# Softmax denominators in a fused attention and state-space kernel: halves of the weight sums added across partitions before the products

## The chip, the cores and the metric

The kernel runs on one core of a Trainium2 chip. The metric is device time in microseconds (us) from launch to end, as the median of a few executions on the chip. A core has five engines with queues of their own: TensorE (PE) for matrix products, VectorE (DVE), ScalarE (ACT), GpSimd (POOL), and SyncE (SP), which here only issues DMAs. Each engine takes its instructions strictly in the order written; between engines, semaphores make an instruction wait for what it needs. PSUM is the memory that TensorE writes to, in eight banks of 128 partitions by 512 fp32 numbers; SBUF is the working memory of 128 partitions.

## What is computed

Cross attention of 4096 queries over 3202 keys with 8 heads of 64, a residual, a layer norm, a linear recurrence with SiLU of 64 states over the 4096 rows, and a second residual with a constant row. All in fp32. Cut to what matters:

```
x      = layernorm(builder_state, g1, beta1)
base_n = layernorm(base_state, g1, beta1)
q, k, v = heads of x, base_n, base_n              # 8 heads of 64
scores = einsum('bhqd,bhkd->bhqk', q, k) / sqrt(64)
attn   = softmax(scores, axis=-1)
out    = einsum('bhqk,bhkd->bhqd', attn, v)
x      = builder_state + out @ W_o.T + b_o
u      = (layernorm(x, g2, beta2) @ W_in.T + b_in) @ Bmat
s      = silu(s @ A.T) + u_t                      # for each row t
return x + states @ Cmat + mod
```

The change concerns the denominator of the softmax alone: the sum over all keys of exp(score), for each query and head.

## The kernel before

**Units and steps.** After a first stage that makes keys and values (up to about 230 us), the work is cut into 64 *units*. A unit is (Q, hp, half): a block Q of 512 queries (eight of them), a pair hp of heads (four), and a half of the block, that is 256 queries (QU). A tile's name carries these three numbers, as acc_2_0_1. The last block takes all pairs of half 0 first and then those of half 1, so the last unit is (7, 3, 1). A unit has 13 *steps* (NDC), one for two chunks of 128 keys (the last one has one chunk).

**A step.** `scores` (L643) makes for both heads (index a) and both chunks (index b) the scores of 128 keys (partitions) by 256 queries, in eight products of 64 by 64 by 256. The array is used as four quarters of 64 rows by 64 columns, so four such products run side by side. The result lies in a PSUM tile `s` of two banks, of which there are two. `weights` (L713) is ScalarE's exp from there into an SBUF tile `p` of 128 x 1024 (18 buffers, the planner's ring "p"). `add` (L721) is VectorE's running sum of the `p` tiles into `acc` (128 keys x 2 heads x 2 chunks x 256 queries, three buffers). `product` (L753) multiplies the weights by the values some four steps later; the halves of its contraction (keys 0 to 63 and 64 to 127 of each chunk) go to two PSUM banks of `po`. 64 keys that do not fill a chunk are handled apart: `sample`, `maximum`, `spread`, `base` (which also find the shift of the exponentials), `extra`, `rest` (L707) and the first products of L741, which have 128 columns.

**The end of a unit** is in `finish`. `output` (L788, ScalarE) copies one bank of `po` to SBUF and `join` (L792, VectorE) adds the other. `fold` (L728, VectorE) adds the two chunks of `acc`. `sums` (L771, TensorE) multiplies by ones: for each head and each half of the partitions one product of 64 by 64 by 256, the two halves to two banks `pd`. `denominators` (L805, ScalarE) reads both banks, copies the first into the SBUF tile `rd`, and sums each over the queries for a check (`rises`). `whole` (L809, VectorE) adds the second bank into `rd`. `inverse` (L812), `scale` (L819) and `fall` (L815), all on VectorE, take the reciprocal, scale the output and sum up for the check. For the last unit `sums` writes to a tile of the `s` ring (pd_last) instead of to two "m" banks.

**What sets the order.** All of this is written as pieces with an engine, a cost, pieces that have to come before, a due time, and the rings (buffers) that a piece takes and gives back. `Plan.order` runs through modelled time and takes on each free engine the ready piece with the earliest due time. `LATE` is how long after its end another engine sees a piece's result; `PORT` lists VectorE's pieces that may not run beside GpSimd's. The order that comes out is the order in every engine's queue. On the chip nothing is reordered: a piece that isn't ready holds up what stands behind it.

**The rings.** "m": two PSUM banks, shared by pd, by the projections (`heads` L320, `outs` L997, `inputs` L1053) and transposes; near the end `first_scan` takes both for the first sweep of the recurrence (za). "s": the two score tiles. "acc": three buffers; a unit's goes back when its `sums` is done. "rd": two buffers.

**The end of the kernel.** Row products (yb, L1343) of the last 256 queries, then two recurrences at once: a sweep over 128 pieces of rows (L1187, L1215, L1222) with its output rows (L1261 to L1286), and one over the last rows (L1425, L1428).

The pieces around the change, before:

Of the kernel before, what the change touches and what calls it, by code (L numbers as in the profile page):

```python
# [10 lines left out]
F32 = mybir.dt.float32  # L11
# [9 lines left out]
P = 128  # L21
TB = 32
# [45 lines left out]
class Plan:  # L68
# [6 lines left out]

    LATE = {"PE": 110, "DVE": 500, "ACT": 110, "POOL": 100, "SP": 5000}
    ENTER, LEAVE = 110, 147
    KEEP, ALONE = 6000, 30000
    PORT = ("add", "rest", "fold", "scale")

# [98 lines left out]
def xattn_ssm_kernel(  # L179
# [545 lines left out]
    def fold(w):  # L725

        acc = w["acc"]
        nc.vector.tensor_tensor(acc[:, :, 0, :], acc[:, :, 0, :], acc[:, :, 1, :], ALU.add)  # L728

    def product(w, c):  # L730

# [30 lines left out]
    def sums(w):  # L762

        if w["last"]:
            both = ps_s.tile([P, 2, 512], F32, tag="s", name="pd_last")
            w["pd"] = [both[:, k] for k in range(2)]
        else:
            w["pd"] = [m_tile([P, 512], f"pd_{w['name']}_{k}") for k in range(2)]
        for a in range(2):
            for k, (k0, k1) in enumerate(((0, HD), (HD, P))):  # L770
                nc.tensor.matmul(  # L771
                    w["pd"][k][a * HD : (a + 1) * HD, :QU],
                    ones[k0:k1],
                    w["acc"][k0:k1, a, 0, :],
                    start=True,
                    stop=True,
                )
# [16 lines left out]
    def finish(w, i, d, plan):  # L794
# [5 lines left out]
        def denominators(k):  # L800
            if k == 0:
                w["rd"] = op.tile([P, QU], F32, tag="rd", name=f"rd_{name}", bufs=2)
            of = rows_of(w, w["pd"][k][:, :QU], True)
            to = of if k else rows_of(w, w["rd"])
            nc.scalar.activation(to, of, AF.Copy, accum_out=rises[:, 3 * i + k : 3 * i + k + 1])  # L805
# [11 lines left out]
        def scale(part):  # L817
# [6 lines left out]
        plan.add(("fold", i), "DVE", 680, partial(fold, w), [("add", i, NDC - 1)], d + 500)  # L824
        plan.add(("sums", i), "PE", 450, partial(sums, w),
                 [("fold", i)] + ([] if last else [from_(d + 2 * STEP)]), d + 1000,
                 ["s"] if last else ["m", "m"], [("acc", ("add", i, 1))], "quarters")
        for k in range(2):
            plan.add(("den", i, k), "ACT", 420, partial(denominators, k), [("den", i, 0) if k else ("sums", i)], d + 2500 + k,
                     [] if k else ["rd"], [(ring, ("sums", i))])  # L830
        plan.add(("whole", i), "DVE", 430, whole, [("den", i, 1)], d + 3000, [], [(ring, ("sums", i))])
        parts = [slice(t * P, (t + 1) * P) for t in range(2)] if last else [slice(0, QU)]
        for t, part in enumerate(parts):
            plan.add(("inverse", i, t), "DVE", 950 if last else 1750, partial(inverse, part),
                     [("whole", i)], d + 5000 + t)
            plan.add(("scale", i, t), "DVE", 400, partial(scale, part),
# [122 lines left out]
    def mixes(Q):  # L959
        return 0 < Q < NQB - 1  # L960
# [588 lines left out]
    def drain(plan):  # L1549
# [14 lines left out]
        plan.add("c2", "SP", 200, open_scan, [("heads", NQB - 1, NC - 1)], a0 - 6 * STEP, ["xn", "q"])  # L1564
        plan.add("open", "DVE", 600, first_scan, ["c2", ("whole", n - 4), *kept_], a0, ["m", "m"])
        for p in sweep("a", None, "end1", a0 + 1000, A_PACE, ["open"]):
            plan.add(*p)
        plan.add("start", "SP", 0, ready_scan, ["fetch", ("sums", n)], d - 2 * STEP, ["s"])
        plan.add("yb", "SP", 0, ready_rows, [("whole", n - 1)], a0, ["m", "m"])
        plan.add("py1", "SP", 0, ready_py, ["start", ("whole", n)], d, ["s"])  # L1570
# [324 lines left out]
```

## Time and profile before

| What | Value |
|---|---|
| Median of 3 runs | 2000.53 us (1997.67 to 2000.59) |
| Profiled execution | 2000.26 us, of which the span of its instructions is 1998.4 |
| Busy share of the span | PE 98%, DVE 72%, ACT 56%, POOL 12% |
| Keys and values, first queries (0 to 231 us) | PE busy 220.2, DVE 59.8, ACT 72.8 |
| Units up to the last block (231 to 1720 us) | PE busy 1483.6, DVE 1177.2, ACT 909.0 |
| Last block (1720 to 1936 us) | PE busy 212.7, DVE 169.4, ACT 128.0 |
| End (1936 to 1998.4 us) | PE busy 43.5, DVE 35.7, ACT 16.7, POOL 25.3 |

How to read the lines of the profile: `L771 PE MATMUL pd<-acc,ones 64*64 64x256 f32 x504 | 38.9, 376 | 0.0` is the group of instructions of line 771 on TensorE that write pd from acc and ones, in a 64 by 64 quarter with 256 columns, 504 of them; they were busy for 38.9 us together, one took 376 ns from its start to its modelled end, and the engine sat idle for 0.0 us before them. Four quarters overlap, and every fp32 product is recorded twice (two passes), so the pace is read from the chain in time, not from one instruction. PEld is the loading of weights into the array. In the chain, "issue" is time in which nothing that the profile shows was waited for.

### The profile page before, as it was taken

How to read it: one execution, taken by the hardware profiler on the slowest of the kernel's cores; microseconds unless marked ns; L12 is line 12 of the kernel's file. 1: busy time of each engine (PE TensorE's matmuls, PEld its weight loads, DVE VectorE, ACT ScalarE, POOL GpSimd, SP SyncE). 2: the span in 40 equal slices, each digit the busy share in tenths (PEclk: the TensorE clock that was granted, in tenths of full speed). 3: DMA queues.
4: the chain of work that ended last, by engine and by line, in shares of the span. 5: the costliest groups of instructions: out<-in, count | busy, mean ns of one | idle time of the engine just before them, and what ended most of it. 6: DMA issues, size and time to landing. Idle time of an engine off the chain costs nothing.

```text
span 1998.4 us, 66546 instructions
## 1 busy us (share of the span) xinstructions
PE 1959.9 (98%) x29070; PEld 1250.2 (63%) x29070; DVE 1442.1 (72%) x1786; ACT 1126.5 (56%) x1478; POOL 235.3 (12%) x378
## 2 busy tenths in 40 slices
PE   8999999999999999999999999999999999999996
PEld 4444566666666666666666666666666666666674
DVE  4311488687877788778868787779777886878675
ACT  2233467566656566556756565656655666655552
POOL 2111000002100120012100210012001100011014
PEclk9999999999999999999999999999999999999998
DMA  5632323223422243224412342234321331544475
GB/s 172 193 98 66 102 80 104 59 81 106 111 74 78 88 113 93 62 71 110 106 48 78 105 109 71 79 95 115 84 78 59 102 92 47 150 136 142 141 209 181
DMA packets 246935, 204.29 MB, mean 102 GB/s; under 512 B 80808, under 2 KB 220072, under 8 KB 246636
## 3 DMA queue, kind: packets, MB, share of 16 engines
q1 hardware_dynamic: 242088, 192.28, 33.3%
q10 hardware_dynamic: 4548, 7.67, 1.2%
q8 instruction: 231, 3.78, 0.8%
q14 instruction: 68, 0.56, 0.1%
HBM read 156.32 MB, written 29.88 MB: 93 GB/s over the span
## 4 chain that ended last, share of the span: by engine, by line
PE 95%; DVE 2%; ACT 1%; issue 1%; DMA 1%; SPq 0%; POOL 0%; ACTq 0%; DVEq 0%; POOLq 0%
PE s L643 35%; PE po L753 34%; PE pq L320 6%; PE pa L997 5%; PE pk L592 4%; PE pv L559 4%; PE pd L771 1%; ACT p L713 1%; PE pu L1053 1%; PE sm L661 1%; PE po L741 1%; PE tp_c L291 0%; PE za L1187 0%; DVE row L1281 0%; PE sm L680 0%
## 5 line engine op out<-in xcount | busy, mean ns | idle before, releaser
L713 ACT ACTIVATE p<-s,shifts 128x1024 f32<-128x1024 f32 (+1 forms) x832 | 885.4, 1080 | 552.2 <-PE s L643 543.4
L721 DVE TENSOR_TENSOR acc<-p,acc 128x1024 f32<-128x1024 f32 (+1 forms) x704 | 842.3, 1196 | 185.5 <-ACT p L713 146.0
L643 PE MATMUL s<-q,k 64*64 64x256 f32 x12800 | 831.4, 378 | 8.6 <-ACT p L713 7.5
L753 PE MATMUL po<-p,v 64*64 64x256 f32 x12800 | 813.3, 376 | 0.0
L643 PEld LDWEIGHTS s<-q,k 64*64 64x64 f32 x12800 | 477.8, 133 | 251.2 <-ACT p L713 54.8
L753 PEld LDWEIGHTS po<-p,v 64*64 64x64 f32 x12800 | 491.1, 133 | 187.8 <-issue 2.4
L991 POOL TENSOR_TENSOR xr<-xr,rowb 128x512 f32<-128x512 f32 x30 | 55.2, 1857 | 892.3 <-DMA xr<-in_x_dram 467.5
L721 DVE TENSOR_TENSOR acc<-p,p 128x1024 f32<-128x1024 f32 x64 | 82.5, 1288 | 69.6 <-ACT p L713 64.0
L320 PE MATMUL pq<-xn,wq 128*128 128x512 f32 x256 | 118.3, 605 | 0.0
L812 DVE RECIPROCAL rd<-rd 128x256 f32<-128x256 f32 (+1 forms) x65 | 112.4, 1729 | 2.2
L997 PE MATMUL pa<-wo,o 128*128 128x512 f32 x240 | 107.0, 599 | 0.0
L559 PE MATMUL pv<-wv,ct 128*128 128x512 f32 (+1 forms) x208 | 95.7, 612 | 1.0 <-DVE wv L375 0.7
L592 PE MATMUL pk<-ct,wk 128*128 128x512 f32 (+1 forms) x224 | 88.8, 549 | 0.0
L1014 POOL TENSOR_TENSOR xr<-x,modb 128x512 f32<-128x512 f32 x30 | 38.1, 1271 | 427.7 <-DVE x L1010 427.7
L527 DVE COPY ct<-tp_c 128x512 f32<-128x512 f32 (+1 forms) x13 | 8.5, 651 | 104.5 <-PE tp_c L291 104.5
L329 ACT ACTIVATE q<-pq,bias 128x512 f32<-128x512 f32 x32 | 22.0, 687 | 108.6 <-PE pq L320 108.6
L320 PEld LDWEIGHTS pq<-xn,wq 128*128 128x128 f32 x256 | 46.0, 189 | 57.6 <-issue 57.5
L997 PEld LDWEIGHTS pa<-wo,o 128*128 128x128 f32 x240 | 44.4, 190 | 56.0 <-issue 55.8
L559 PEld LDWEIGHTS pv<-wv,ct 128*128 128x128 f32 (+1 forms) x208 | 38.1, 192 | 44.4 <-issue 42.2
L592 PEld LDWEIGHTS pk<-ct,wk 128*128 128x128 f32 x224 | 39.2, 190 | 42.6 <-issue 42.6
L707 DVE TENSOR_TENSOR acc<-x,acc 2x256 f32<-2x256 f32 x128 | 61.4, 480 | 2.9
L600 ACT ACTIVATE ks<-pk,bias 128x512 f32<-128x512 f32 (+1 forms) x28 | 18.0, 642 | 75.4 <-PE pk L592 68.3
(214 smaller groups left out, 1133.6 us busy)
## 6 DMA issues: line engine op xcount, KB each, us to landing
k<-kd SPq DMA_DIRECT2D x432, 128.0 KB, 2.2
v<-vd SPq DMA_DIRECT2D x432, 128.0 KB, 2.3
xn<-x SPq DMA_DIRECT2D x416, 32.0 KB, 1.9
xr<-in_x_dram SPq DMA_DIRECT2D x30, 256.0 KB, 3.4
x1d<-xr SPq DMA_DIRECT2D x30, 256.0 KB, 2.9
x<-in_x_dram SPq DMA_DIRECT2D x28, 256.0 KB, 3.8
cx<-in_ctx_dram SPq DMA_DIRECT2D x25, 256.0 KB, 3.0
vd<-vs SPq DMA_DIRECT2D x25, 256.0 KB, 2.4
```

Of the source, the lines that this page charges most:

```text
L320: nc.tensor.matmul(pq, wq[:, i, hp * P : (hp + 1) * P], xn[:, i, :], start=(i == 0), stop=(i == NC - 1),)
L559: nc.tensor.matmul(pv[h * HD : h * HD + n, :H], ct[:, k, o : o + n], wv[:, k, :], start=(i == 0), stop=(i == NC // parts - 1), skip_group_ ...
L592: nc.tensor.matmul(pk[:, :n_g], wk[:, i, hp * P : (hp + 1) * P], ct[:, i, :n_g], start=(i == 0), stop=(i == NC - 1),)
L643: nc.tensor.matmul(s[k0 : k0 + HD, a, b, :], kts[(*w["at"][:2], c)][r, b * CK + k0 : b * CK + k0 + HD], q[r], start=True, stop=True, skip_ ...
L707: nc.vector.tensor_tensor(to[r], t[r], to[r], ALU.add)
L713: nc.scalar.activation(t[:, :, :nb, :], w["ps"][c][:, :, :nb, :], AF.Exp, bias=w["shift"])
L721: nc.vector.tensor_tensor(w["acc"][:, :, :nb, :], t[:, :, :nb, :], before[:, :, :nb, :], ALU.add)
L753: nc.tensor.matmul(w["po"][a * HD : (a + 1) * HD, k, :QU], vts[Q, hp, c][r, b, a * HD : (a + 1) * HD], t[r, a, b, :], start=(c == 0 and b ...
L812: nc.vector.reciprocal(w["rd"][:, part], w["rd"][:, part])
L991: nc.gpsimd.tensor_tensor(v["x"], v["x"], rowb, ALU.add)
L997: nc.tensor.matmul(v["pa"], o_t[Q, c, half][:, t * P : (t + 1) * P], wo[:, c, :], start=(c == 0), stop=(c == NC - 1),)
L1014: nc.gpsimd.tensor_tensor(v["x"], v["x1"], modb, ALU.add)
```

## The change

For all units but the last, the halves of the sums over keys are added before the products, crosswise: partitions 0 to 63 (k = 0) collect the first 128 queries and partitions 64 to 127 (k = 1) the other 128. `swap` copies with ScalarE each half's missing part from the other 64 partitions into a tile of the "rd" ring; `gather` adds it with VectorE into `acc`. `sums` then has 128 columns in each product, and each bank of pd holds whole denominators of 128 queries, so `denominators` reads 128 columns from each bank straight into `rd` and `whole` falls away. `sums` may start from the ninth step of the next unit on (8 * STEP) instead of from the third, and the pieces that waited for `whole` wait for the second `denominators`. In the planner, VectorE's `LATE` is 300 instead of 500, and `gather` joins `PORT`.

```
-    LATE = {"PE": 110, "DVE": 500, "ACT": 110, "POOL": 100, "SP": 5000}
+    LATE = {"PE": 110, "DVE": 300, "ACT": 110, "POOL": 100, "SP": 5000}
...
-    PORT = ("add", "rest", "fold", "scale")
+    PORT = ("add", "rest", "fold", "gather", "scale")
...
+    def halves(w, k):
+        return slice(k * HD, (k + 1) * HD), w["acc"][:, :, 0, k * P : (k + 1) * P]
+
+    def swap(w):
+        t = op.tile([P, QU], F32, tag="rd", name=f"swap_{w['name']}", bufs=2)
+        w["swap"] = t.rearrange("p (a j) -> p a j", a=2)
+        for k in range(2):
+            r, of = halves(w, k)
+            nc.scalar.copy(w["swap"][r], of[(1 - k) * HD : (2 - k) * HD])
+
+    def gather(w):
+        for k in range(2):
+            r, of = halves(w, k)
+            nc.vector.tensor_tensor(of[r], w["swap"][r], of[r], ALU.add)
...
             for k, (k0, k1) in enumerate(((0, HD), (HD, P))):
+                of = slice(0, QU) if w["last"] else slice(k * P, (k + 1) * P)
                 nc.tensor.matmul(
-                    w["pd"][k][a * HD : (a + 1) * HD, :QU],
+                    w["pd"][k][a * HD : (a + 1) * HD, of],
                     ones[k0:k1],
-                    w["acc"][k0:k1, a, 0, :],
+                    w["acc"][k0:k1, a, 0, of],
...
-            of = rows_of(w, w["pd"][k][:, :QU], True)
-            to = of if k else rows_of(w, w["rd"])
+            of, to = rows_of(w, w["pd"][k][:, :QU], True), rows_of(w, w["rd"])
+            if last:
+                to = of if k else to
+            elif mixes(w["at"][0]):
+                of, to = (t[:, :, k * P // 2 // TB : (k + 1) * P // 2 // TB] for t in (of, to))
+            else:
+                of, to = (t[:, k * P : (k + 1) * P] for t in (of, to))
...
-        plan.add(("sums", i), "PE", 450, partial(sums, w),
-                 [("fold", i)] + ([] if last else [from_(d + 2 * STEP)]), d + 1000,
+        if not last:
+            plan.add(("swap", i), "ACT", 760, partial(swap, w), [("fold", i)], d + 600, ["rd"])
+            plan.add(("gather", i), "DVE", 860, partial(gather, w), [("swap", i)], d + 700, [],
+                     [("rd", ("swap", i))])
+        plan.add(("sums", i), "PE", 450 if last else 300, partial(sums, w),
+                 [("fold", i)] if last else [("gather", i), from_(d + 8 * STEP)], d + 1000,
...
-            plan.add(("den", i, k), "ACT", 420, partial(denominators, k), [("den", i, 0) if k else ("sums", i)], d + 2500 + k,
+            plan.add(("den", i, k), "ACT", 580 if last else 450, partial(denominators, k), [("den", i, 0) if k else ("sums", i)], d + 2500 + k,
...
-        plan.add(("whole", i), "DVE", 430, whole, [("den", i, 1)], d + 3000, [], [(ring, ("sums", i))])
+        if last:
+            plan.add(("whole", i), "DVE", 430, whole, [("den", i, 1)], d + 3000, [], [(ring, ("sums", i))])
...
-                     [("whole", i)], d + 5000 + t)
+                     [("whole", i) if last else ("den", i, 1)], d + 5000 + t)
```

In `drain`, the opening of the scan and the row products' banks (`open`, `yb`) wait for `("den", ..., 1)` of a unit where they waited for its `whole`.

## The prediction

> **What bounds the kernel now.** I read the page's span and chain first, then the groups with shapes kept apart, then the chain in time around the products that are narrowed, and last its end. Durations are in microseconds (us) unless a row says ns.
>
> ```profile
> span 1998.4 us, 66546 instructions
> PE 95%; DVE 2%; ACT 1%; issue 1%; DMA 1%; SPq 0%; POOL 0%; ACTq 0%; DVEq 0%; POOLq 0%
> ```
>
> TensorE is the bound: 95% of the chain that ended last. Whatever shortens its stream shortens the kernel, as long as no score (L643) waits longer for ScalarE to empty one of the two score buffers.
>
> ```profile
> L713 ACT ACTIVATE p<-s,shifts 128x1024 f32<-128x1024 f32 x768 | 842.1, 1113 | 540.3 <-PE s L643 532.1
> L721 DVE TENSOR_TENSOR acc<-p,acc 128x1024 f32<-128x1024 f32 x640 | 797.0, 1245 | 178.2 <-ACT p L713 145.6 <-DVE acc L721 0.5
> L771 PE MATMUL pd<-acc,ones 64*64 64x256 f32 x504 | 38.9, 376 | 0.0
> L809 DVE TENSOR_TENSOR rd<-pd,rd 128x256 f32<-128x256 f32 x63 | 26.3, 417 | 17.7 <-ACT pd L805 16.2
> L741 PE MATMUL po<-x,vx 64*64 64x128 f32 x512 | 26.1, 270 | 0.0
> L805 ACT ACTIVATE pd<-pd 128x256 f32<-128x256 f32 x63 | 24.5, 389 | 0.0
> L788 ACT COPY o<-po 128x256 f32<-128x256 f32 x64 | 23.4, 365 | 3.4 <-PE po L753 3.4
> L866 ACT ACTIVATE xh_y<-x,nm_y,rstd_y 128x512 f32<-128x512 f32 x30 | 22.9, 808 | 0.0
> ```
>
> x504 is 63 units times eight matmul records (four products, two passes each); the last unit is apart and stays as it was. The chain in time around one unit's denominators, then at three scores in a row:
>
> ```profile
> 1045.46 0.22 PE po L741 x8
> 1045.68 0.43 PE po L753 x8
> 1046.11 1.73 PE s L643 x32
> 1047.84 0.43 PE pd L771 x8
> 1048.27 1.04 PE s L643 x16
> ```
>
> ```profile
> 694.58 0.91 PE s L643 x16
> ...
> 695.57 1.12 ACT p L713
> ...
> 696.74 1.09 PE s L643 x16
> ```
>
> Columns: start, length, what. Eight records of 256 columns take 0.43, eight of 128 columns 0.22. A score of 16 records is 0.86 undisturbed; the one behind pd took 1.04, so it waited 0.18. Behind two scores it needs the exponentials of the first, 1.12 plus hand-over; a third score in a row therefore loses about 0.63 (696.74 less 694.58, less twice 0.865, plus the 0.2 that the third one still runs long).
>
> **The change, part by part.** *Narrower products* (63 units): 128 columns for 256. By the L741 row 0.22 for 0.43, so 63 x 0.215 = 13.5 less TensorE time. The other end: if eight weight loads (0.37 for eight of pd, in the row of the weight loads) were not hidden behind the matmuls in front, pd would take 0.37 and save 63 x 0.06 = 3.8. I take 0.22, as L741 is the same form with as many loads, between the same neighbours.
>
> The Trainium skill, "TensorE: Matmul & The Clock Gate", sections "Back-to-back issue gap" and "LDWEIGHTS (loading the stationary operand)", speaks against this: spacing is set by load and matmul together, and a load takes its columns divided by 1.2 in ns, by which eight loads of 64 columns one behind another are 0.43 (an estimate from that page) and nothing at all would be saved. The trace disagrees: L741's eight went by in 0.22.
>
> *Copies on ScalarE* (two, 64 partitions x 256, SBUF to SBUF; no such row). From below L788, 0.365 from PSUM; from above L866, 0.81 for twice the columns from SBUF. I take 0.40, as the size is L788's. The two readings of pd shrink from 0.385 to about 0.27 (0.587 for 512 columns in the row of L572, 0.365 for 256: 0.87 ns a column). So 2 x 0.40 - 2 x 0.11 = 0.58 more per unit, 37 in all on an engine that is 56% busy. The cover is ScalarE's idle time before a weight pass:
>
> ```profile
> 272.50 1.11 ACT L713 ACTIVATE p<-s,shifts 128x1024 f32<-128x1024 f32 x1 [0.61 <-PE s L643]
> ```
>
> 0.61 idle per step; two copies of 0.80 put the next weight pass 0.19 late, and the score that waits for it comes three TensorE groups later (3 x 0.865 = 2.6, against 0.17 + 1.11 + 0.19). So the copies cost nothing where scores and products alternate. At 0.81 apiece they still would. Without cover, 0.58 x 63 = 37.
>
> *Fold before the copies.* The copies wait for VectorE's fold (L728), and every weight pass stands in line behind them. I matched the changed order's place of each pair with the trace of before: in 62 of 63 units the fold had ended at least 0.24 before the weight pass in front of the copies ended; in one it is 0.2 late. In seven units the changed order puts a reciprocal with its followers (2.6) ahead of the fold; there the copies stand 4.3 behind the fold's old end. So nothing is taken for this wait.
>
> *Gather in, whole out, on VectorE.* Two adds of 256 columns (0.42, L819; the L707 rows have 0.42 median, 0.48 mean) for one (L809, 0.42): 0.42 more per unit, 26 in all, on an engine that is 72% busy. VectorE waits in the gather for the copies, and adds queue behind it; they free weight buffers, of which there are 18. Up to the last unit that costs nothing.
>
> *The order* moves far beyond these lines, since the planner now takes 300 ns for VectorE's lateness and holds the products back to step 8. I counted in both orders the places where a score comes too soon behind the score before last. Before: 16 threes in a row (0.63), 44 "score, score, pd, score" (0.12 mean) and 17 "score, sample, product, score" (0.12): 10.1 + 5.3 + 2.0 = 17.4. After: 21, none, 31, and 24 "score, pd, product, half score, score", whose slack is 1.51 against some 1.6 (0.1 each): 13.2 + 3.7 + 2.4 = 19.3. Changes between quarter and full array: 142 in both. So 1.9 is given back.
>
> *The last unit.* Here VectorE, not TensorE, sets the end:
>
> ```profile
> 1935.58 0.70 DVE acc L728
> 1936.28 0.14 issue
> 1936.42 0.66 PE pd_last L771 x8
> 1937.08 4.50 PE yb L1343 x10
> ```
>
> The changed order holds three things against it. The scan's opening takes both "m" banks before unit 7_0_1 has its denominators, so that unit's reciprocal, scaling and rise check (1.79 + 0.45 + 0.36 = 2.6 with gaps) fall into the last unit, beside those of 7_1_1 and 7_2_1 that were there already. Its sums keep the third "acc" buffer until pd of 7_0_1, behind score 5, so the first add of the last unit, at 1910.85 before, waits to about 1916.4 (the weights of step 5 began at 1916.2). And the last unit's join stands ahead of its last four adds. From 1916.4 by rows: add 1.28 and two rests 0.95; group 2.6; add 1.28; group 2.6; five adds 6.4; group 2.6; add 1.28; join 0.42; three and a half adds 4.5; fold 0.7: 1941.0, against 1936.3 before: 4.7 later. Given back: the row products of heads 1 and 2 now stand before pd_last, so from the fold's end to the scan it is 5.7 (4.8 to the second scaling, 0.9 for its product) instead of 6.1: 0.4. Net 4.3. Ends: 0, if what remained of VectorE's queue ran while TensorE is still busy, and 5.5. The final scan's two chains are woven differently with the same instructions; I take 0 and plus or minus 1.5.
>
> Sum: -13.5 + 1.9 + 4.3 = -7.3. The profiled execution took 2000.26 (span 1998.4 and 1.9 around it), so 1993.0; the median of the runs, 2000.53, gives 1993.2. I say 1993.
>
> **The rivals.**
> *The end absorbs its queue*: -13.5 + 1.9 = -11.6: 1989. For it: TensorE still has 5 of row products to do after the last unit's products. Against: the chain runs through fold, pd_last and the reciprocal anyway.
> *ScalarE's line (slower)*: copies stand where the fold is not yet done, and the weight passes behind them hold up the scores. The slack in the alternating stretch is 2.6 - 1.28 - 0.80 = 0.5. At a mean wait of 0.8 for the fold each unit loses 0.3: 63 x 0.3 = 19, less 7.3: 2012. It decides from 0.12 lost per unit (7.3 / 63). For it: VectorE gets 26 more work, the gather makes it wait for ScalarE, so that each in turn waits for the other. Against: the 62 of 63 above. The Trainium skill, "TensorE: Matmul & The Clock Gate", section "Architectural detail: the array is 16× 32×32, not 1× 128×128", says that ScalarE's and VectorE's queues are strictly first in, first out; the trace agrees in that L713 alone stands between a late score and TensorE (0.63 above).
> *Weight loads bind*: pd takes 0.37: -3.8 + 1.9 + 4.3: 2002.7. Against: L741.
> *Waits a little dearer everywhere*: 4 to 5 more over 63 units, 1998: the planner reckons 1061 ns for a weight pass that takes 1113.
>
> **How the numbers follow.** Forecast 0.52, its own range 1989.5 to 1996.5. End absorbed 0.20. Dearer waits 0.10. ScalarE's line 0.14. Loads 0.04. The range reaches from below the absorbed end, 1985.5, to 2002, over the dearer waits and to the loads' case; it leaves out most of ScalarE's line and little below. 0.2% (4 us) is about what a measurement tells from no change: faster, under 1996.5, is the forecast, the absorbed end and a part of the dearer waits, 0.76; same (1996.5 to 2004.5) 0.11; slower 0.13.
>
> **What would show it.** The chain gives pd 0.22 for x8; in the groups, copies of 0.37 to 0.45 and pd readings near 0.27; ScalarE at 58%, VectorE at 74%. Scores' waits stay near 19 in sum. In the last unit the fold ends some 4.7 later after the last score than before. Wrong would be: ScalarE idle before the copies, released by VectorE, or scores waiting in the middle of units; or pd at 0.37.

## The result, and the profile after

| Kernel | Median | Runs | Ratio to before, 95% interval |
|---|---|---|---|
| before | 1998.97 us (1997.46 to 2000.65) | 14 | |
| after | 2004.64 us (1998.63 to 2010.64) | 14 | 1.0028 [1.0016, 1.0040] |

The kernel became 0.28% slower; the forecast was 1993.0. Its runs spread over 12 us, those of the kernel before over 3. The profiled execution after took 2009.5 (span 2007.7), at the slow end of that spread; the same kernel was profiled again later at 2006.2 (span 2004.4), and where the two differ both are given.

First the page of the kernel after: span, busy time of each engine, and the row of the copies.

```profile
span 2007.7 us, 66572 instructions
...
PE 1958.0 (98%) x29070; PEld 1241.9 (62%) x29070; DVE 1462.4 (73%) x1849; ACT 1163.2 (58%) x1604; POOL 215.3 (11%) x378
...
L740 ACT COPY swap<-acc 64x256 f32<-64x256 f32 x126 | 51.1, 405 | 20.7 <-DVE acc L728 18.0
```

Then the groups of the kernel after with shapes kept apart (busy us, mean ns of one, idle before them and what ended it):

```profile
L745 DVE TENSOR_TENSOR acc<-swap,acc 64x256 f32<-64x256 f32 x126 | 53.7, 426 | 8.0 <-ACT swap L740 5.4
...
L728 DVE TENSOR_TENSOR acc<-acc 128x512 f32<-128x512 f32 x64 | 46.1, 721 | 2.0
...
L828 ACT ACTIVATE rd<-pd 128x128 f32<-128x128 f32 x126 | 33.8, 278 | 9.8 <-PE pd L789 9.7
...
L789 PE MATMUL pd<-acc,ones 64*64 64x128 f32 x504 | 25.4, 269 | 0.0
```

Every price is where the prediction had it: copies 0.405 (0.40), readings 0.278 (0.27), gather 0.426 (0.42), products 269 ns a record, where they were 376 before. What was not expected stands at the end of the L740 row: ScalarE stood idle for 18.0 us in front of the copies until VectorE's fold was done. The view of the fold's own line says how often:

```profile
L728 DVE TENSOR_TENSOR acc<-acc x64: 681/691/1649, 246.4 to 1944.6; 128x512 f32<-128x512 f32 x64
...
  ACT swap L740: 18.0, 22
```

22 times out of 63, and in the second profile 23 times, 21.4 us. The fold itself took 1649 ns at the longest (min/median/max 681/691/1649); before, 694 was its longest.

One such place in time, in the kernel after, the first unit of block 1 (start, length, what, in brackets the idle time before it and what ended it):

```profile
426.27 2.96 POOL L1019 TENSOR_TENSOR xr<-xr,rowb 128x512 f32<-128x512 f32 x2 [108.78 <-DMA v<-vd]
426.34 1.76 DVE L721 TENSOR_TENSOR acc<-p,acc 128x512 f32<-128x512 f32 x1
...
428.13 1.65 DVE L728 TENSOR_TENSOR acc<-acc 128x512 f32<-128x512 f32 x1
...
428.54 0.40 PE L758 MATMUL po<-x,vx 64*64 64x128 f32 x8
...
429.19 1.04 PE L643 MATMUL s<-q,k 64*64 64x256 f32 x16
...
429.87 0.83 ACT L740 COPY swap<-acc 64x256 f32<-64x256 f32 x2 [1.70 <-DVE acc L728]
430.73 1.12 ACT L713 ACTIVATE p<-s,shifts 128x1024 f32<-128x1024 f32 x1
...
431.90 1.09 PE L643 MATMUL s<-q,k 64*64 64x256 f32 x16 [1.67 <-ACT p L713]
```

The fold runs beside an addition of GpSimd's (L1019) and takes 1.65; the unit's last add (L721) ran beside one too and took 1.76, where such an add takes 0.73 in the mean of its row. So VectorE stands some 2 us behind. ScalarE has nothing but the copies at the head of its queue and stands still for 1.70. The weight pass (L713) behind them, whose scores were done long before, starts at 430.73; the score that needs its buffer starts 1.67 late. TensorE had come there fast: the short products of L758, half a product, and a pair of scores with no product between.

How much this is, from the traces: five blocks of queries (40 units, from the first weight pass of block 1 to that of block 6). A wait is the time between the starts of two groups on TensorE, less the first one's columns at their undisturbed pace; the level of such a count hangs on the pace taken, the differences between kernels hardly do.

| Kernel (us) | Five blocks | Waits | of them: second score of the pair behind L758 | of them: products |
|---|---|---|---|---|
| before | 1074.7 | 26.2 | 0 | 3.1 |
| after, first profile | 1076.9 | 37.1 | 7.9 | 7.8 |
| after, second profile | 1078.5 | 38.7 | 10.3 | 7.5 |

The narrowing is worth 40 x 0.215 = 8.6 here, and it is there in full: in 62 of the 63 units, in both profiles, the group behind pd starts 0.22 after it. It was saved, and given back in waits: 1074.7 - 8.6 + (37.1 - 26.2) = 1077.0 against 1076.9, and 1078.6 against 1078.5. (As waits are counted, that sum has to come out; it only shows that nothing else changed.) The last weight pass starts at 1933.8 and 1934.9 in the two profiles, 1930.2 before, so it came 3.6 and 4.7 later, where 11.6 sooner was forecast. The five blocks are 2.2 and 3.8 of that; before them 4.2 and 2.7 are lost, behind them 2.7 and 1.8 gained, and these stretches were not taken apart.

The other loss is at the end. Before and after, in windows of 10 us (busy us of PE, PEld, DVE, ACT, POOL, then TensorE's granted clock, share of DMA, GB/s). Before:

```profile
1940.00:1950.00 10.00, 7.61 (x38) 3.70 (x36) 5.45 (x13) 3.21 (x7) 5.39 (x10) 0.86 0.87 245
1950.00:1960.00 10.00, 9.77 (x109) 6.69 (x112) 3.88 (x12) 2.68 (x8) 2.28 (x4) 0.80 0.10 37
```

After:

```profile
1940.00:1950.00 10.00, 4.94 (x18) 1.85 (x16) 7.91 (x12) 0.95 (x4) 0.00 (x0) 0.89 1.04 274
1950.00:1960.00 10.00, 7.90 (x32) 3.37 (x31) 4.68 (x12) 2.52 (x6) 5.37 (x10) 0.67 0.19 69
1960.00:1970.00 10.00, 10.00 (x112) 7.29 (x112) 3.12 (x11) 3.28 (x8) 1.39 (x2) 0.76 0.04 14
```

The last fold ended 11.5 after the start of the last weight pass (1945.29 less 1933.82), before it was 6.1 (1936.27 less 1930.18): 5.4 later, where 4.7 was forecast. TensorE is idle for half of a window here, and then its clock is at two thirds; before it was at 0.86 and 0.80. From the last fold to the end of the span it is 62.1 before, 62.4 after, and 58.5 in the second profile after.

### The profile page after: what moved, and what is told of

The parts are those of the page before. It is cut to its first block, busy times and chain, and to the rows that moved or that the text cites. A ratio compares the mean times of both kernels' runs of the same rounds, so it can differ in the third digit from the quotient of the medians.

```text
span 2007.7 us, 66572 instructions
## 1 busy us (share of the span) xinstructions
PE 1958.0 (98%) x29070; PEld 1241.9 (62%) x29070; DVE 1462.4 (73%) x1849; ACT 1163.2 (58%) x1604; POOL 215.3 (11%) x378
## 5 line engine op out<-in xcount | busy, mean ns | idle before, releaser
L713 ACT ACTIVATE p<-s,shifts 128x1024 f32<-128x1024 f32 (+1 forms) x832 | 888.7, 1085 | 526.0 <-PE s L643 518.7
L721 DVE TENSOR_TENSOR acc<-p,acc 128x1024 f32<-128x1024 f32 (+1 forms) x704 | 843.4, 1198 | 267.2 <-ACT p L713 235.9
L643 PE MATMUL s<-q,k 64*64 64x256 f32 x12800 | 833.4, 379 | 13.9 <-ACT p L713 11.6
L770 PEld LDWEIGHTS po<-p,v 64*64 64x64 f32 x12800 | 480.8, 133 | 202.3 <-issue 12.8
L1019 POOL TENSOR_TENSOR xr<-xr,rowb 128x512 f32<-128x512 f32 x30 | 49.4, 1657 | 931.9 <-DMA xr<-in_x_dram 664.4
L320 PE MATMUL pq<-xn,wq 128*128 128x512 f32 x256 | 119.1, 608 | 0.0
L721 DVE TENSOR_TENSOR acc<-p,p 128x1024 f32<-128x1024 f32 x64 | 82.3, 1286 | 7.2 <-ACT p L713 7.0
L320 PEld LDWEIGHTS pq<-xn,wq 128*128 128x128 f32 x256 | 46.3, 191 | 58.4 <-issue 58.3
L740 ACT COPY swap<-acc 64x256 f32<-64x256 f32 x126 | 51.1, 405 | 20.7 <-DVE acc L728 18.0
```

Of the source, the lines that this page charges most:

```text
L320: nc.tensor.matmul(pq, wq[:, i, hp * P : (hp + 1) * P], xn[:, i, :], start=(i == 0), stop=(i == NC - 1),)
L643: nc.tensor.matmul(s[k0 : k0 + HD, a, b, :], kts[(*w["at"][:2], c)][r, b * CK + k0 : b * CK + k0 + HD], q[r], start=True, stop=True, skip_ ...
L713: nc.scalar.activation(t[:, :, :nb, :], w["ps"][c][:, :, :nb, :], AF.Exp, bias=w["shift"])
L721: nc.vector.tensor_tensor(w["acc"][:, :, :nb, :], t[:, :, :nb, :], before[:, :, :nb, :], ALU.add)
L740: nc.scalar.copy(w["swap"][r], of[(1 - k) * HD : (2 - k) * HD])
L770: nc.tensor.matmul(w["po"][a * HD : (a + 1) * HD, k, :QU], vts[Q, hp, c][r, b, a * HD : (a + 1) * HD], t[r, a, b, :], start=(c == 0 and b ...
```

## The experiments

**First: the two halves of the change apart.** Four kernels ran together; the kernel before took 1998.63 beside them.

*Only narrower products*, in the kernel before:

```
-                    w["pd"][k][a * HD : (a + 1) * HD, :QU],
+                    w["pd"][k][a * HD : (a + 1) * HD, : QU if w["last"] else P],
...
-                    w["acc"][k0:k1, a, 0, :],
+                    w["acc"][k0:k1, a, 0, : QU if w["last"] else P],
...
```

Not shown are the lines by which ScalarE and VectorE read those 128 columns twice, so that their work keeps its size.

> The kernel before, but in 63 units the products for the denominators take the first 128 of the 256 columns only, and ScalarE's two readings take those 128 twice, so that ScalarE, VectorE and the order of the work stay as they were (left out: the sums over the other 128 queries). Theory (the copies on ScalarE and the gather delay the weight pass, the narrow products work): the eight product records of a unit take about 0.22 us instead of 0.43, but in 44 of 63 units they stand just ahead of a score that waits for ScalarE anyway, so only the other 19 units save it: about 19 x 0.21 = 4 us, ratio 0.998. Rival (the products' time is TensorE's own in every unit): 63 x 0.215 = 13.5 us less, ratio 0.993. Second rival (narrow products give nothing): 1.000.

1994.29, ratio 0.9977 [0.9968, 0.9986]: 4.3 less, as the theory had it. In 44 of 63 units the group behind the products still starts late, for it is a score that waits for ScalarE; there the products only fill the wait.

*The planner's constant alone*, in the kernel before:

```
-    LATE = {"PE": 110, "DVE": 500, "ACT": 110, "POOL": 100, "SP": 5000}
+    LATE = {"PE": 110, "DVE": 300, "ACT": 110, "POOL": 100, "SP": 5000}
```

> The kernel before with only the planner's VectorE constant LATE set to 300 as in the kernel after; nothing is left out. Theory (the loss comes from the copies): within 2 us of the kernel before, ratio 0.999 to 1.001. Rival (the other order of VectorE's work is what costs): 1.004 or more.

1995.42, 0.9984 [0.9975, 0.9993]: 3.2 less, outside what either theory said. Five blocks take 1074.5 as before; of the 3.2 by which the last weight pass comes sooner, 2.5 are gained in the last block. So a new order alone moves the time by some us.

*No copies*, in the kernel after:

```
-            nc.scalar.copy(w["swap"][r], of[(1 - k) * HD : (2 - k) * HD])
+            pass
...
-            nc.vector.tensor_tensor(of[r], w["swap"][r], of[r], ALU.add)
+            nc.vector.tensor_tensor(of[r], of[r], of[r], ALU.add)
```

> The kernel after without ScalarE's 126 swap copies: the gather adds a tile to itself (left out: the crosswise sums), everything else in its order. Theory (the copies of 0.40 us stand ahead of weight passes for which scores wait): TensorE's waits for the weight passes between 231 and 1552 us fall from 43 us back to about 30, and the time by 10 to 15 us against the kernel after, to about 1990 to 1994, ratio to the kernel before 0.995 to 0.9975. Rival (the copies lie in ScalarE's idle time and cost nothing, as the prediction took it): no change against the kernel after, ratio 1.002 to 1.004.

1997.87, 0.9999 [0.9990, 1.0008]: 6.8 less than after. So in this order the copies do cost, though not 10. The waits behind L758 are down to 1.3 in five blocks, but those of products are up to 9.6, and 32.3 are left in all.

*The last block's sums sooner*, in the kernel after:

```
-                 [("fold", i)] if last else [("gather", i), from_(d + 8 * STEP)], d + 1000,
+                 [("fold", i)] if last else [("gather", i), from_(d + (2 if w["at"][0] == NQB - 1 else 8) * STEP)], d + 1000,
```

> The kernel after, but the sums of the last block of queries may be placed from two steps after the unit's weights instead of eight; nothing is left out. Theory (about 5 us of the loss come from the end, where the denominators of the last units' neighbours are read, inverted and scaled in one heap ahead of the last fold): the inverse of the unit before last moves ahead by tens of us, the last fold ends about 4 us sooner after the last scores, and the time falls by 4 to 6 us against the kernel after, to about 1999, ratio to the kernel before 0.998 to 1.001. Rival (the last fold waits for its own unit's weights in any case): no change, ratio 1.002 to 1.004.

1997.70, 0.9995 [0.9986, 1.0004]: 6.9 less than after. The reciprocal of unit 7_0_1 starts at 1864.2 instead of 1923.9, and the last fold ends 5.5 after the start of the last weight pass instead of 11.5. The loss at the end is thus what the prediction described.

**Second: after again, and the copies on another engine.** Beside these four, the kernel before took 1999.14.

> The kernel after once more, nothing is left out. Its 14 runs so far spread over 12 us (1998.6 to 2010.6), those of the kernel before over 3. Theory (the heap of late denominators ahead of the last fold leaves TensorE idle at the end, and its clock is taken back by different amounts): a median of 2002 to 2006 again with the same spread, and the last fold ends 11 to 12 us after the last weight pass starts whatever the time. Rival (the profiled execution was an unlucky one, and most of the loss is not in the kernel): a median under 2000, ratio under 1.001.

2004.96, 1.0026 [1.0016, 1.0036]: the loss is the kernel's.

*The constant back to 500, in the kernel after:*

```
-    LATE = {"PE": 110, "DVE": 300, "ACT": 110, "POOL": 100, "SP": 5000}
+    LATE = {"PE": 110, "DVE": 500, "ACT": 110, "POOL": 100, "SP": 5000}
```

> The kernel after with the planner's VectorE constant LATE at 500 as in the kernel before; nothing is left out. Theory (300 gains some 3 us by its order in the kernel before, and would do so here): 2 to 5 us more than the kernel after, 2005 to 2010, ratio to the kernel before 1.003 to 1.006. Rival (the order that 300 brings is itself at fault here): under 2001, ratio under 1.001.

2010.60, 1.0060 [1.0048, 1.0072]: 300 helps here too, by 5.6.

*Copies on GpSimd:*

```
-            nc.scalar.copy(w["swap"][r], of[(1 - k) * HD : (2 - k) * HD])
+            nc.gpsimd.tensor_copy(w["swap"][r], of[(1 - k) * HD : (2 - k) * HD])
...
-            plan.add(("swap", i), "ACT", 760, partial(swap, w), [("fold", i)], d + 600, ["rd"])
+            plan.add(("swap", i), "POOL", 1400, partial(swap, w), [("fold", i)], d + 600, ["rd"])
```

> The kernel after with the swap copies on GpSimd in place of ScalarE; nothing is left out. By the rows GpSimd's copies should take 0.5 to 0.7 us each, some 70 to 90 us over the span, on an engine that is idle for 89% of it. Theory (the copies on ScalarE cost what leaving them out gave back, about 7 us): the waits of scores behind product groups fall as without the copies, and the time by 4 to 7 us against the kernel after, ratio to the kernel before 0.999 to 1.001. Rival (what counted was that the gather waited for nothing, and a slower copy is later still, or GpSimd and VectorE slow each other): no change or more, ratio 1.002 or above.

1990.13, 0.9956 [0.9943, 0.9969]: 14.5 less than after, twice what leaving the copies out gave. That can't be the copies' own time alone; the plan has changed with them.

*Both, GpSimd's copies and the sooner sums, by the two edits above:*

> The kernel after with the swap copies on GpSimd and the sums of the last block from two steps after the unit's weights; nothing is left out. Theory (two separate losses, copies in ScalarE's line and the heap at the end): both gains add, 10 to 13 us less than the kernel after, 1991 to 1995, ratio to the kernel before 0.9955 to 0.998. Rival (they are one loss, seen twice): no better than the sooner sums alone, ratio 0.999 to 1.000.

1987.86, 0.9943 [0.9931, 0.9956]. Better than either kernel; but the sooner sums give 2.3 here and not 6.9, so the two gains don't simply add.

**Third: order and engine crossed.** The planner is told one engine, and the copies are issued on the other. TensorE's and VectorE's order is then the same, line for line, as that of the partner. The kernel before took 1998.37.

```
-            plan.add(("swap", i), "ACT", 760, partial(swap, w), [("fold", i)], d + 600, ["rd"])
+            plan.add(("swap", i), "POOL", 1400, partial(swap, w), [("fold", i)], d + 600, ["rd"])
```

> The order of work on TensorE and VectorE that the plan with GpSimd's copies gave, but the copies issued by ScalarE; nothing is left out. Theory (the copies' own time in ScalarE's line costs what leaving them out gave, 7 us, and the order that the plan makes round them costs the other 8): 1996 to 1998, ratio 0.998 to 1.0. Rival (it is the order alone): 1990 to 1991, ratio 0.9955 to 0.996. Second rival (it is the copies alone): 2003 to 2006, ratio 1.002 to 1.004.

1990.23, 0.9965 [0.9952, 0.9978].

```
-            nc.scalar.copy(w["swap"][r], of[(1 - k) * HD : (2 - k) * HD])
+            nc.gpsimd.tensor_copy(w["swap"][r], of[(1 - k) * HD : (2 - k) * HD])
```

> The order of work on TensorE and VectorE of the kernel after, but the copies issued by GpSimd; nothing is left out. Theory (two parts, as above): as with no copies at all, 1997 to 1999, ratio 0.999 to 1.0. Rival (the order alone): 2003 to 2006. Second rival (the copies alone): 1990 to 1991.

2003.74, 1.0032 [1.0019, 1.0044]. The theory of two parts falls: the order decides, the engine doesn't. The copies in themselves are free in a good order, as the prediction said; in the order of the kernel after there is a loss on either engine, only elsewhere. With GpSimd's copies nothing waits behind L758 (0.4). But GpSimd's additions now stand behind its copies and run beside two small adds of VectorE (L707), which take 2.82 together, where the kernel after shows 0.84; so VectorE empties the product's bank (L810) late. The row of the products in that kernel, and the first unit of block 1:

```profile
L770 PE MATMUL po<-p,v 64*64 64x256 f32 x12800 | 816.3, 377 | 7.2 <-DVE o L810 7.2
```

```profile
427.36 2.92 POOL L1019 TENSOR_TENSOR xr<-xr,rowb 128x512 f32<-128x512 f32 x2
...
427.75 2.82 DVE L707 TENSOR_TENSOR acc<-x,acc 2x256 f32<-2x256 f32 x2
...
430.60 0.42 DVE L810 TENSOR_TENSOR o<-po,o 128x256 f32<-128x256 f32 x1
...
431.08 1.74 PE L770 MATMUL po<-p,v 64*64 64x256 f32 x28 [1.04 <-DVE o L810]
```

The same happens in the first unit of each of the five blocks, and by the count of waits it costs 1.21 each time.

And the same place in the order planned for GpSimd, with ScalarE's copies:

```profile
422.66 1.65 DVE L728 TENSOR_TENSOR acc<-acc 128x512 f32<-128x512 f32 x1
422.73 1.88 PE L320 MATMUL pq<-xn,wq 128*128 128x512 f32 x4
...
425.36 0.83 ACT L740 COPY swap<-acc 64x256 f32<-64x256 f32 x2
...
427.19 0.40 PE L758 MATMUL po<-x,vx 64*64 64x128 f32 x8
...
427.83 1.91 PE L643 MATMUL s<-q,k 64*64 64x256 f32 x32
```

The fold runs just as long beside GpSimd, but TensorE is at a projection (L320) meanwhile. (The rest of this order differs too, so that this is why it costs nothing is argued, not isolated.) The fold is over at 424.31, the copies start 1.05 later and wait for nothing, and the pair of scores runs through (x32 in 1.91).

*Products narrow and whole at the later place*, in the kernel before, without copies and gather; both with this edit, the first also with the half products of the first experiment:

```
-    LATE = {"PE": 110, "DVE": 500, "ACT": 110, "POOL": 100, "SP": 5000}
+    LATE = {"PE": 110, "DVE": 300, "ACT": 110, "POOL": 100, "SP": 5000}
...
-                 [("fold", i)] + ([] if last else [from_(d + 2 * STEP)]), d + 1000,
+                 [("fold", i)] + ([] if last else [from_(d + 8 * STEP)]), d + 1000,
```

> The kernel before with LATE 300, its sums from eight steps after the unit's weights as in the kernel after, and the half products of the first experiment (left out: the sums over 128 of the 256 queries); no copies, no gather. Now 24 of the 63 units have their products between two pairs of scores (44 in the kernel before). Theory (the narrowing saves 0.215 us only where no score behind waits for ScalarE): 39 x 0.215 = 8.4 us less than the kernel beside it with whole products. Rival (it saves the same 4 us wherever the products stand). Second rival (0.215 us in each unit): 13.5 us less.

> The same as the kernel beside it with products of 256 columns; nothing is left out, and TensorE's and VectorE's order is the same. Theory: the heap of late denominators at the end costs its 5 us here too, and LATE 300 gives its 3: 1998 to 2002, ratio 0.9995 to 1.0015. Rival (the later place has no price at the end): 1995 to 1996, ratio 0.998.

2005.49 (1.0035 [1.0022, 1.0048]) and 2013.30 (1.0073 [1.0060, 1.0086]). The difference, 7.8, agrees with the 8.4 of the theory within the runs' spread: the narrowing pays where no score behind waits anyway. But the whole products at this place cost 14.9 against the kernel before, not 0 to 3. Holding the sums back to step 8 is not cheap by itself; its last fold is 5.4 further behind the last weight pass than before (11.5), and in five blocks it loses 5.5. Of these, 3.9 are five waits of products, 0.40 to 1.07 each, in the first units of the blocks; each stands behind pieces of VectorE (the last add, the fold, a scaling) that ran beside GpSimd's additions and took up to 1.66 instead of 0.42 to 0.69.

**Fourth: only the copies' place.** What in the order? The copies get an earliest time, and the sums another step. The kernel before took 1999.28.

```
-            plan.add(("swap", i), "ACT", 760, partial(swap, w), [("fold", i)], d + 600, ["rd"])
+            plan.add(("swap", i), "ACT", 760, partial(swap, w), [("fold", i), from_(d + 2 * STEP)], d + 600, ["rd"])
```

> The kernel after with ScalarE's swap copies not before the score two steps after the unit's end, which puts them behind the fifth weight pass of the next unit (56 of 63) instead of the first to fourth; nothing is left out. Theory (the copies stand where TensorE needs the next weight pass at once, between the last product of the old unit and a pair of scores): the waits of that pair, 9 to 12 us between 231 and 1552 us in the kernel after, fall under 2 us, and the time to 1990 to 1995, ratio to the kernel before 0.9955 to 0.998. Rival (orders of this planner differ by more than 10 us by chance, and the copies' place decides nothing): 2001 to 2008.

2003.87, 1.0023 [1.0014, 1.0032].

With three steps:

```
-            plan.add(("swap", i), "ACT", 760, partial(swap, w), [("fold", i)], d + 600, ["rd"])
+            plan.add(("swap", i), "ACT", 760, partial(swap, w), [("fold", i), from_(d + 3 * STEP)], d + 600, ["rd"])
```

> The same with three steps, behind the sixth weight pass in all 63 units; nothing is left out. Theory: as with two steps, 1990 to 1996, since the next product group and scores leave ScalarE room there too. Rival (every other place meets another tight group): 2001 or more.

1998.54, 0.9998 [0.9989, 1.0007].

Two steps for the copies as above, and two for the sums of the last block:

```
-                 [("fold", i)] if last else [("gather", i), from_(d + 8 * STEP)], d + 1000,
+                 [("fold", i)] if last else [("gather", i), from_(d + (2 if w["at"][0] == NQB - 1 else 8) * STEP)], d + 1000,
```

> The copies behind the fifth weight pass, and the sums of the last block from two steps instead of eight; nothing is left out. Theory (the two losses are apart): 2 to 6 us less than with the copies moved alone, 1986 to 1992, ratio 0.994 to 0.997, and the last fold ends 5 to 6 us after the last weight pass starts instead of 11 to 12. Rival: no further gain.

1998.26, 0.9997 [0.9988, 1.0005].

Nine steps for the sums, the copies as in the kernel after:

```
-                 [("fold", i)] if last else [("gather", i), from_(d + 8 * STEP)], d + 1000,
+                 [("fold", i)] if last else [("gather", i), from_(d + 9 * STEP)], d + 1000,
```

> The kernel after with the sums from nine steps after the unit's weights in place of eight, which leaves the copies where they were (34 of 63 behind the first to third weight pass) and moves the rest of the order a little; nothing is left out. Theory (the copies' place is the cause): still 2001 to 2008, ratio 1.0015 to 1.005. Rival (the order of the kernel after is an unlucky one among like ones): under 1998.

2001.25, 1.0008 [1.0000, 1.0017]. In both kernels with moved copies the waits behind L758 are gone as expected (0.4 in five blocks), and ScalarE no longer waits for the fold. But the times are not the 1990 to 1996 of the theory: with three steps 6.1 was gained, with two 0.8, which the intervals don't tell from nothing, as the rival had it. The loss moved on to the products: they wait 11.9 and 10.9 in five blocks, 7.8 in the kernel after. In the kernel after no single wait of a product is over 0.1; now one in the first unit of each block is 0.57 to 0.97, and 0.58 to 1.09 with three steps, for the bank that VectorE empties in L810, together 4.1 and 4.4. Each time pieces of VectorE had run beside GpSimd's additions shortly before, as at 425.5 with two steps, where the last add took 1.60 and the fold 1.65. The gather, which now waits for the copies (8.2 and 31.3 us), isn't what holds L810 up: in both kernels it stands behind its unit's L810, 63 times of 63. The sooner sums give 5.6 again, as expected. With nine steps the time is at the edge of the theory's range, and the waits behind L758 fall to 5.4.

**Fifth: the collision with GpSimd, and the best version.** The kernel before took 1998.64.

```
-                nc.gpsimd.tensor_tensor(v["x"], v["x"], rowb, ALU.add)
+                pass
```

> The kernel after without GpSimd's 30 additions of a row to the residual (left out: that row), the order on the other engines the same. In the kernel after, up to five of the seven first folds of a block ran 1.65 us instead of 0.69, each beside one of these additions, and ScalarE stood in front of the copies behind them. Theory (that collision is a part of the loss and the source of its spread): every fold takes 0.69, the waits of the pair of scores behind the copies fall from 9 to 12 us to 5 or less, and the time by 3 to 7 us against the kernel after, to 1998 to 2002, with runs within 5 us of each other. Rival (the copies wait for the fold as long anyway): 2003 to 2006 and the same spread.

1998.30, 0.9997 [0.9989, 1.0006]: 6.3 less than after. Every fold takes 0.69, ScalarE waits for it for 11.6 (16 times), and the waits behind L758 are 3.3 in five blocks, where they were 7.9 and 10.3; the five blocks are 5.1 and 6.7 shorter. So GpSimd's additions account for about half of the waits that the kernel after has over the kernel before (10.9 and 12.5); 5.8 stay without them. But the runs still spread from 1994.7 to 2004.5, where 5 us were expected, so the spread is not from there alone.

The best order, with ScalarE's copies:

```
-            plan.add(("swap", i), "ACT", 760, partial(swap, w), [("fold", i)], d + 600, ["rd"])
+            plan.add(("swap", i), "POOL", 1400, partial(swap, w), [("fold", i)], d + 600, ["rd"])
...
-                 [("fold", i)] if last else [("gather", i), from_(d + 8 * STEP)], d + 1000,
+                 [("fold", i)] if last else [("gather", i), from_(d + (2 if w["at"][0] == NQB - 1 else 8) * STEP)], d + 1000,
```

> The order planned for GpSimd's copies with the sums of the last block from two steps, the copies issued by ScalarE as in the kernel after; nothing is left out. Theory (the order decides, the copies' engine does not, and the end is a loss apart): within 2 us of the same order with GpSimd's copies, 1986 to 1990, ratio 0.994 to 0.9955. Rival (ScalarE's copies cost something of their own): 1992 or more.

1987.69, 0.9951 [0.9939, 0.9963]: the changed kernel, copies on ScalarE, with two entries in the plan altered, is 0.5% faster than the kernel before.

The five blocks once more, in us; the third column is what the narrowing and the waits make of the 1074.7 before (less 8.6, plus the waits less 26.2), a check on the count and no more:

| Kernel | Five blocks | Worked out | Waits | behind L758 | products |
|---|---|---|---|---|---|
| no copies | 1072.1 | 1072.2 | 32.3 | 1.3 | 9.6 |
| after's order, GpSimd's copies | 1075.6 | 1075.7 | 35.8 | 0.4 | 13.8 |
| copies two steps on | 1073.3 | 1073.4 | 33.5 | 0.4 | 11.9 |
| copies three steps on | 1068.4 | 1068.5 | 28.6 | 0.4 | 10.9 |
| no GpSimd rows | 1071.8 | 1071.9 | 32.0 | 3.3 | 7.5 |
| GpSimd's order, ScalarE's copies | 1064.8 | 1064.9 | 25.0 | 0.2 | 6.0 |

## Why the prediction was wrong

**The step that failed** is the one headed *Fold before the copies*: "in 62 of 63 units the fold had ended at least 0.24 before the weight pass in front of the copies ended", hence "nothing is taken for this wait". It set the changed order's copies against the times of a trace made in the old order. In the new one ScalarE waited for the fold 22 and 23 times, 18.0 and 21.4 us. In the old trace no fold was lengthened by an addition of GpSimd's (the longest took 0.694); in the new order two and five folds were, and there the waits were dearest. Without those additions ScalarE still waits 16 times, 11.6, but the pair behind L758 loses only 3.3. A sign of it stood in the prediction's own rows, in L707's mean of 0.48 over its median of 0.42: the long ones ran beside GpSimd's additions. The second half of the failure is the count of score waits: +1.9 was forecast for 63 units, which is 1.2 for 40; measured are +10.9 and +12.5. Of these 7.9 and 10.3 stand at one kind of place, the pair of scores behind L758, which the count did not list. By the prediction's prices the second score of that pair has 1.51 (0.22 for L758, 0.43 for half a product, 0.865 for a score) for a weight pass that needs 0.17 + 1.11. That was enough before, where nothing is lost; with a late fold and the copies ahead of the weight pass it was not. Waits of products are another 4.7 and 4.4, each under 0.1, and other waits fell by 1.7 and 2.2.

**The rival that came true** is *ScalarE's line*, given 0.14. Its mechanism was right: copies that stand where the fold isn't done, and weight passes and scores late behind them. Its price was not. It put 0.3 on each unit, 19 us and 2012 in all; behind L758 it is 7.9 / 40 = 0.20 and 0.26 per unit in the mean, and that is near by chance, for the loss is not spread evenly: of the waits behind L758, 6.2 of 9.1 and 9.7 of 12.5 us (from 222 to 1711 us) lie in the first unit of a block, up to 1.85 at a time. The rival did not name what made the fold late there, GpSimd's additions, and neither did any other. Its objection, the 62 of 63, was the very number that failed. Of the signs named for being wrong, "ScalarE idle before the copies, released by VectorE" is what the row of L740 shows.

**Right:** the prices of the copies, the readings, the gather and the products; TensorE's saving of 13.5 (8.6 of 8.6 in five blocks); and that the copies cost nothing where ScalarE has its 0.61 per step, which the order planned for GpSimd shows with ScalarE's copies. There the last weight pass starts at 1916.9, 13.3 before the 1930.2 of the kernel before, where -11.6 was forecast, and its median is 8.1 under that of the kernel before, where -7.3 was. The loss at the end was right in place and nearly in size (5.4 and 4.9 for 4.7); what it then costs differs with the clock, below.

**Left open:** the good order differs from that of the kernel after in more than the copies' place, and moving that alone did not reach it. VectorE is held up by GpSimd in the good order too (five folds of 1.64), and there neither the pair behind L758 nor a product waits over 0.1 in five blocks; which of its differences brings that was not isolated. Nor was the good order run without GpSimd's additions. The 5.8 of waits that the kernel after keeps without them, and what it loses ahead of the five blocks, were not taken apart.

## What to carry to other kernels

When a plan rewrites the order, times read from the old trace don't tell what will be ready in the new one: a piece that makes one in-order engine wait for another has to be priced with the place it gets, at the tightest spot that it meets, not with the mean slack. A small operation put at the head of a busy queue is free or dear by the order round it; try two or three places (here by a larger cost in the plan) before judging the idea. Look for pieces that take longer than their median, too: a wait for another engine can stand inside an instruction, and no row of idle time then shows it. And a gain in a filler, work done while the next step waits anyway, is no gain until the filler stands elsewhere.

## What was not expected of the hardware

**GpSimd holds up VectorE.** Seven folds in the two profiles of the kernel after ran beside an addition of GpSimd's (L1019) and took 1.64 to 1.76 us instead of 0.69; in the place shown above GpSimd's additions end at 429.23 and the fold at 429.78, 0.55 later, and at 1289.05 it is 0.55 again (1288.59 + 1.56 = 1290.15, against 1290.70), as in the other five. Adds are stretched in the same way, as the 1.76 and the 2.82 above, and were so in the kernel before (1.23 in the median and 2.35 at the longest in the line of L721), where no product waited over 0.1 in the five blocks. GpSimd starts when a DMA lands, so the planner's rule against running the two side by side did not hold on the chip. The Trainium skill, "SBUF — State Buffer", section "Who interferes with whom", says that a VectorE instruction with two inputs in SBUF and a GpSimd instruction that reads SBUF hold a shared pair of ports one at a time, each for its whole length. The traces agree: 0.55 of a fold's 0.69 is left when the addition ends, and the two folds that began ahead of an addition beside them (644.38, the addition 644.62; in the second profile 1723.61 and 1724.10) took 0.69.

**The same idle time, another clock.** In both profiles of the kernel after, TensorE is busy for about 5 of the 10 us from 1940 on (4.94 and 5.39). In the first the clock then is 0.67 and 0.76 over 20 us; in the second, whose windows follow, it is 0.87 and 1.00 (0.95 ahead of that, 0.89 in the first):

```profile
1940.00:1950.00 10.00, 5.39 (x19) 2.20 (x19) 7.95 (x11) 0.95 (x4) 0.00 (x0) 0.95 1.06 255
1950.00:1960.00 10.00, 7.72 (x42) 3.22 (x43) 5.17 (x13) 3.64 (x8) 5.38 (x10) 0.87 0.57 153
1960.00:1970.00 10.00, 8.82 (x138) 6.57 (x138) 5.59 (x18) 2.66 (x9) 3.85 (x6) 1.00 0.27 92
```

From the last scaling to the end of the span it is 57.6 us (2007.7 less 1950.06) in the first and 53.7 (2004.4 less 1950.69) in the second: 3.9 between two executions of one order. By the rows, the three windows lose 6.8 us of full clock in the first and 1.8 in the second, so the clock can account for it; that it is the cause is argued. The runs go with it in part: those of the kernel after at a mean clock of 0.995 or 0.996 took 1998.6 to 2006.2, those at 0.992 from 2008.3 on. Idle time at the end alone doesn't bring the spread: with GpSimd's copies and the sums from eight steps the last fold also ended 10.9 after the start of the last weight pass, and five runs lay within 1.5. With the last block's sums sooner the spread was 6.1 us, and 1.0 with GpSimd's copies too; with ScalarE's in that order five of six runs lay within 2.5 and one, at 0.992, was 5.7 above them. The Trainium skill, "TensorE: Matmul & The Clock Gate", says in Part 1, on the clock gate, that the window in which TensorE's activity is judged runs freely, so that one kernel meets it at another phase each time. That would give such a spread, but no run here shows the window.
